# Two ternary feed-forward loops: one slot list, source order on four engines, squares moved to GpSimd and ACT, the norm's root mean square from its variance

## The chip, the cores and the metric

The kernel runs on one core of one Trainium2 chip. The time is the device time of one execution in microseconds (us). Four executions of the kernel before took 2186.79, 2187.14, 2192.76 and 2193.71 us, a median of 2189.95. A further execution was recorded by the hardware profiler; it took 2197.59 us. The engines are named as in the profile: PE (TensorE, matmuls), DVE (VectorE), ACT (ScalarE), POOL (GpSimd) and SP (SyncE, which here only issues DMAs). "PEld" is PE's loading of weights.

## The reference

`x` is 2048 tokens by 256 in float32. The reference adds eight layers to it, one after the other, each of them on the layer norm of `x`: four rounds of an attention over a context of 1601 rows and a feed-forward layer. Two of the four feed-forward layers have ternary weights, and these two are the case.

The second round's (L1, `ffn1` in the kernel):

```
def _bitlinear(x, w_latent):
    scale = jnp.clip(jnp.mean(jnp.abs(w_latent), axis=1, keepdims=True), 1e-05, None)
    tern = jnp.clip(jnp.round(w_latent / scale), -1.0, 1.0)
    ...
    return x @ (w * scale).T
h = _bitlinear(x, w_fc) + gate * (x @ v.T @ fast_b.T @ u.T)
r = jnp.maximum(h, 0.0)
return _bitlinear(r * r, w_proj)
```

It goes from 256 to 1024 columns and back, with a term of rank 16 in the first product and a squared relu between the two.

The third round's (L2, `ffn2`):

```
def _ternary_linear(x, w):
    ...
    rms = jnp.sqrt(jnp.sum(x * x, axis=-1, keepdims=True)) / jnp.sqrt(jnp.asarray(d, x.dtype))
    x_norm = x / (rms + EPS)
    return jnp.einsum('bsd,fd->bsf', x_norm, w_q)
h = jax.nn.gelu(_ternary_linear(x, w_up), approximate=False)
return _ternary_linear(h, w_down)
```

The same sizes; each of the two products first divides its input's rows by their root mean square (EPS is 1e-8). What the layer receives is already the layer norm `(x - mean) / sqrt(var + 1e-5)`. So the root mean square of the first product's input is close to one, and it follows from the variance: the mean square of a normed row is `var / (var + 1e-5)`.

## The kernel before

**Chunks and slots.** The tokens stay in SBUF as 16 tiles of 128 x 256. Both layers work through four chunks of 512 tokens (four tiles). Inside a chunk a loop runs over the 1024 hidden columns, two blocks of 128 at a time: four passes, which this text calls slots. A slot has an *up* part and a *down* part. Up multiplies the normed chunk (columns on the partitions) by the weights of two blocks into a PSUM tile of two banks (`psc`, two such tiles); then come the nonlinearity and the split of its result; down multiplies the split result back to 256 columns and adds it into two PSUM banks (`pa`, two such banks) that collect a whole chunk.

**The split.** The matmuls here take their operands in a rounded float32 form (`F32R`, fp32r in the profile). To keep the precision, a value is split into its rounded form `hi` and the rest `lo`, and each product is done for both. `parts` (L1101) splits the hidden values: ACT writes `rhi` (L1106), then DVE writes `rlo` (L1107) as the difference. The norm's output is split in the same way into `xnhi` (ACT, L179) and `xnlo` (DVE, L180). So an up has eight matmuls of 512 columns in `ffn2` (L1174), and ten in `ffn1` (L1078 and, for the term of rank 16, L1082); a down has sixteen of 256 columns (L1115).

**The norm** (`norm_steps`, L133) of a chunk takes DVE's statistics of four tiles (`bn_stats`, `bn_aggr`, L139 and L140), POOL's reciprocal root of the variance (an add L144 and a pow L145 on 128 x 4), DVE's four `xn` (L151), PE's eight transposes (L173), and the split. It is a generator: it yields at several points, so that a caller may spread it over a loop with `step(gen, n)`; `norm` (L126) runs it to its end at once. With `rms=True`, which only `ffn2` asks for, ACT squares the four `xn` with a row sum (L161), POOL and DVE make the inverse root of it (`rms_inverse`, L185: a pow, a scale, a DVE reciprocal), and DVE multiplies the four `xn` by it (L164).

**ffn1's loop** (from L1066). After an up, ACT takes the relu of the two halves (L1085), DVE squares the result in place (L1086), and `parts` splits it. The down of a slot is issued when more than two slots are waiting for theirs; the downs left over are issued at the end of the chunk. The next chunk's whole norm and its product of rank 16 (`low_rank`, L1047: eight matmuls L1052, two ACT copies, one DVE difference, `y4`) are issued behind the up of the second slot. At the end of the chunk DVE scales the four tiles of the accumulators (L1098, `y1`, three buffers) and POOL adds them to `x` (L1099).

**ffn2's loop** (from L1162). After an up, ACT takes the gelu of both halves (L1179) and `parts` splits it. DVE squares it (L1183 for the first slot, in place at L1185 for the others), and POOL sums the squares of the slots (L1186). The downs and the next norm are issued as in `ffn1`. At the end of the chunk eight matmuls against a column of ones sum the squares over the partitions (L1197), DVE copies the sums (L1202), `rms_inverse` inverts their root, and DVE scales the accumulators and adds them to `x` in one operation a tile (L1206).

**What sets the order.** The program is written in a framework that schedules each engine's instructions by priority from a planned timeline, and inserts the semaphores. `tc.manual_schedule(engines=...)` keeps the engines that it names to the order of the source for the instructions inside it. Before the change both layers name PE alone:

```
s.enter_context(tc.manual_schedule(engines={mybir.EngineType.PE}))
```

DVE, ACT and POOL are then ordered by the planner; instructions of other stages, which are outside, may stand between theirs. Each engine executes its queue in order.

Of the kernel before, what the change touches and what calls it, by code (L numbers as in the profile page):

```python
# [8 lines left out]
F32 = mybir.dt.float32  # L9
BF16 = mybir.dt.bfloat16  # L10
F32R = mybir.dt.float32r
AF = mybir.ActivationFunctionType
ALU = mybir.AluOpType
AX = mybir.AxisListType

P = 128
D = 256
IN_ORDER = {mybir.EngineType.PE, mybir.EngineType.Activation, mybir.EngineType.DVE, mybir.EngineType.Pool}
# [3 lines left out]
CH = 512  # L22
NCH = NTOK // CH
TPC = CH // P
# [16 lines left out]
def drain(gen):  # L41
    if gen is not None:
        for _ in gen:
            pass


def step(gen, n):
    if gen is None:
        return
    for _ in range(n):  # L50
        if next(gen, True):
            return


class Net:
# [77 lines left out]
    def norm_steps(self, c, out, row_scale=None, rms=False, split=None):  # L133

        nc = self.nc
# [9 lines left out]
        nc.gpsimd.tensor_tensor(rstd, rstd, self.mhalf, ALU.pow)  # L145
        if row_scale is not None:
            nc.gpsimd.tensor_tensor(rstd, rstd, row_scale, ALU.mult)
        xns = []
        for i in range(TPC):
            xn = self.xnp.tile([P, D], F32, name="xn", bufs=4)  # L150
# [3 lines left out]
            xns.append(xn)  # L154
            if i == 1:
                yield
        if rms:
            ss = self.small.tile([P, TPC], F32, name="ss")
            for i in range(TPC):
                sq = self.xnp.tile([P, D], BF16, name="sq", bufs=1)  # L160
                nc.scalar.activation(sq, xns[i], AF.Square, accum_out=ss[:, i : i + 1])  # L161
            ri = self.rms_inverse(ss, D)
            for i in range(TPC):
                nc.vector.tensor_scalar(xns[i], xns[i], ri[:, i : i + 1], None, ALU.mult)  # L164
        yield
        if split is None:
            xnT = self.xnp.tile([P, 2, CH], F32, name="xnT")
# [789 lines left out]
    def ffn1(self):  # L957
# [7 lines left out]
        with ExitStack() as s:  # L965
# [81 lines left out]
            def low_rank(hi, lo):  # L1047
# [11 lines left out]
                nc.vector.tensor_tensor(y4[64:P], ps[64:P], top[64:P].bitcast(F32), ALU.subtract)  # L1059
                return y4  # L1060

            def inputs(c):
                hi, lo = self.norm(c, split=hp)
                return hi, lo, low_rank(hi, lo)

            s.enter_context(tc.manual_schedule(engines={mybir.EngineType.PE}))  # L1066
            nxt = inputs(0)
            for c in range(NCH):
                hi, lo, y4 = nxt
                acc = [self.pa() for _ in range(2)]  # L1070
                late = []
                for f in range(0, NF, 2):
                    ps = self.psc()
                    for k in range(2):
                        fs = slice((f + k) * P, (f + k + 1) * P)
                        for kc in range(2):
                            for n, part in enumerate((hi, lo)):
                                nc.tensor.matmul(  # L1078
                                    ps[:, k, :], lhsT=wfT[:, kc, fs], rhs=part[:, kc, :],
                                    start=kc == 0 and n == 0, stop=False,  # L1080
                                )
                        nc.tensor.matmul(ps[:, k, :], lhsT=b4[:, fs], rhs=y4, start=False, stop=True)  # L1082
                    r = tp.tile([P, 2, CH], F32, name="r1")
                    for k in range(2):
                        nc.scalar.activation(r[:, k, :], ps[:, k, :], AF.Relu, scale=sc1[:, f + k : f + k + 1])  # L1085
                    nc.vector.tensor_tensor(r, r, r, ALU.mult)  # L1086
                    parts = self.parts(hp, r)
                    late.append((f, parts))
                    if len(late) > 2:
                        self.down(acc, *late.pop(0), wpT, NF)  # L1090
                    if f == 2 and c + 1 < NCH:
                        nxt = inputs(c + 1)
                for f, parts in late:
                    self.down(acc, f, parts, wpT, NF)
                for i in range(TPC):
                    x = self.x[c * TPC + i]
                    y = tp.tile([P, D], F32, name="y1")
                    nc.vector.tensor_tensor(y, acc[i // 2][:, i % 2 * D : (i % 2 + 1) * D], scb, ALU.mult)  # L1098
                    nc.gpsimd.tensor_tensor(x, x, y, ALU.add)  # L1099

    def parts(self, pool, r):  # L1101

# [19 lines left out]
    def ffn2(self):  # L1122
        tc, nc, a = self.tc, self.nc, self.a
        F = 1024
# [6 lines left out]
        with ExitStack() as s:  # L1131
# [27 lines left out]
            wdT = pool.tile([P, NF, D], F32R, name="wdT")  # L1159
            self.transpose_down(wdT, tdn)  # L1160

            s.enter_context(tc.manual_schedule(engines={mybir.EngineType.PE}))  # L1162
            nxt = self.norm(0, rms=True, split=hp)
            for c in range(NCH):
                hi, lo = nxt
                acc = [self.pa() for _ in range(2)]
                sq = hp.tile([P, 2, CH], F32, name="sq2")
                late = []
                for f in range(0, NF, 2):
                    ps = self.psc()  # L1170
                    for k in range(2):
                        for kc in range(2):
                            for n, part in enumerate((hi, lo)):
                                nc.tensor.matmul(  # L1174
                                    ps[:, k, :], lhsT=wuT[:, kc, (f + k) * P : (f + k + 1) * P], rhs=part[:, kc, :],
                                    start=kc == 0 and n == 0, stop=kc == 1 and n == 1,
                                )
                    h = tp.tile([P, 2, CH], F32, name="h2")
                    nc.scalar.activation(h, ps, AF.Gelu)  # L1179
                    parts = self.parts(hp, h)  # L1180

                    if f == 0:
                        nc.vector.tensor_tensor(sq, h, h, ALU.mult)  # L1183
                    else:
                        nc.vector.tensor_tensor(h, h, h, ALU.mult)  # L1185
                        nc.gpsimd.tensor_tensor(sq, sq, h, ALU.add)  # L1186
                    late.append((f, parts))
                    if len(late) > 2:
                        self.down(acc, *late.pop(0), wdT, NF)
                    if f == 2 and c + 1 < NCH:  # L1190
                        nxt = self.norm(c + 1, rms=True, split=hp)
                for f, parts in late:
                    self.down(acc, f, parts, wdT, NF)
                ps = self.pm()
                for i in range(TPC):
                    for k in range(2):
                        nc.tensor.matmul(  # L1197
                            ps[:, i : i + 1], lhsT=sq[:, k, i * P : (i + 1) * P], rhs=self.ones[:, 0:1],
                            start=k == 0, stop=k == 1,
                        )  # L1200
                ss = self.small.tile([P, TPC], F32, name="ss2")
                nc.vector.tensor_copy(ss, ps[:, :TPC])  # L1202
                ri = self.rms_inverse(ss, F)
                for i in range(TPC):
                    x = self.x[c * TPC + i]
                    nc.vector.scalar_tensor_tensor(  # L1206
                        x, acc[i // 2][:, i % 2 * D : (i % 2 + 1) * D], ri[:, i : i + 1], x, ALU.mult, ALU.add
                    )


    def attention3(self):
# [583 lines left out]
```

## Time and profile before

| what | value |
|---|---|
| median of four executions | 2189.95 us |
| profiled execution, its own time | 2197.59 us |
| its span, first to last instruction | 2195.9 us |
| mean granted PE clock | 0.944 of full |
| busy in the span: PE, DVE, ACT, POOL | 1939.2, 1202.6, 715.8, 629.8 us |
| relus of `ffn1` (L1085), first and last start | 1233.5 and 1325.0 us |
| gelus of `ffn2` (L1179), first and last start | 1637.2 and 1729.6 us |
| ACT's squares in the norm (L161) | 16, median 418 ns, and 187 ns each for reading the sum |
| DVE's squares, `ffn1` (L1086) and `ffn2` (L1185) | 16, median 1225 ns; 12, 1212 to 3317 ns |
| POOL's sums of squares (L1186) | 12, 2338 to 3257 ns |

How to read it: a line such as `L1086 DVE TENSOR_TENSOR r<-r 128x1024 f32` names the line of the kernel, the engine, the operation, and the tiles that it writes and reads. Times in the timeline are from the span's start. In a table of waits, "PE pm L1052 <- DVE xnlo L180: 13.0, 4, 4.1" says that PE's instructions of line 1052 waited 13.0 us in total, in 4 places, at most 4.1 us, for what DVE does in line 180. In a table of stretches a row gives its length, the busy time and number of instructions of each engine, and then the clock that was granted to PE, as a share of full. A matmul's duration reaches beyond the start of the next one, since they are pipelined; the distance of starts is what counts.

### The profile page before, as it was taken

The numbers are of one execution on the slowest core, as the hardware profiler recorded it, in microseconds if no ns is written. First come the engines' busy times: TensorE is split into PE (matmuls) and PEld (weight loads), VectorE is DVE, ScalarE is ACT, GpSimd is POOL, SyncE is SP. The second block draws the span as 40 slices with busy tenths as digits, with TensorE's granted clock in tenths as the row PEclk, the third lists the DMA queues.
The fourth block names the chain that finished last, engine by engine and source line by source line (L and its number), as shares of the span: only waits on it lengthen the run. The fifth ranks groups of instructions, "written<-read, shape, count | busy, mean of one in ns | idle before, by whom it ended". The sixth has DMA issues, their size and how long they took to land.

```text
span 2195.9 us, 22805 instructions
## 1 busy us (share of the span) xinstructions
PE 1939.2 (88%) x8841; PEld 965.5 (44%) x8841; DVE 1202.6 (55%) x2252; ACT 715.8 (33%) x968; POOL 629.8 (29%) x405
## 2 busy tenths in 40 slices
PE   7789999999998587789898789999977879888899
PEld 3223333333333533234444575455566622333487
DVE  4655655556462499985645553322156558677400
ACT  4544434444443100000011443111133246555422
POOL 1168878778686000000000111000013300111210
PEclk9799999999998599999999799999988889999999
DMA  8820000000000000000200100000000000000261
GB/s 283 274 77 1 1 1 1 1 1 1 1 1 1 0 1 0 1 0 0 67 1 2 39 1 22 1 0 1 0 1 1 5 1 1 1 1 1 102 203 62
DMA packets 39698, 63.51 MB, mean 29 GB/s; under 512 B 5133, under 2 KB 32158, under 8 KB 39582
## 3 DMA queue, kind: packets, MB, share of 16 engines
q1 hardware_dynamic: 37776, 60.33, 8.4%
q10 hardware_dynamic: 1806, 1.64, 0.2%
q8 instruction: 71, 1.16, 0.2%
q14 instruction: 45, 0.37, 0.1%
HBM read 59.87 MB, written 2.10 MB: 28 GB/s over the span
## 4 chain that ended last, share of the span: by engine, by line
PE 66%; DVE 20%; ACT 5%; issue 4%; DMA 3%; POOL 2%; SPq 0%; ACTq 0%; DVEq 0%; POOLq 0%
PE pa L468 7%; PE psc L456 5%; PE psc L641 5%; PE psc L780 4%; PE pa L800 4%; DVE ge L590 4%; DVE mp L381 4%; PE psc L1578 3%; DVE ge L592 3%; PE psc L1716 3%; PE pa L1727 3%; DVE ri L418 2%; ACT p L1585 2%; PE psc L454 2%; PE pm L376 2%
## 5 line engine op out<-in xcount | busy, mean ns | idle before, releaser
L477 POOL TENSOR_TENSOR sp<-sp,p 128x1024 f32<-128x1024 f32 (+1 forms) x176 | 419.0, 2381 | 62.4 <-ACT p L461 51.9
L381 DVE TENSOR_REDUCE mp<-pm 128x1 f32<-128x512 f32 x384 | 242.8, 680 | 162.5 <-PE pm L376 161.8
L461 ACT ACTIVATE p<-psc 128x1024 f32<-128x1024 f32 (+1 forms) x208 | 212.9, 1024 | 261.4 <-PE psc L456 162.2
L456 PE MATMUL psc<-qT,kT 64*128 64x512 f32 (+1 forms) x832 | 220.2, 592 | 0.0
L468 PE MATMUL pa<-p,v 128*64 128x512 f32 (+1 forms) x832 | 202.8, 609 | 0.0
L607 PE MATMUL psc<-ge,pick 128*8 128x512 bf16 x512 | 142.3, 378 | 37.8 <-DVE ge L590 19.0
L1585 ACT ACTIVATE p<-psc 100x1024 f32<-100x1024 f32 x128 | 124.0, 1022 | 75.8 <-PE psc L1578 73.1
L1564 DVE TENSOR_REDUCE ms<-psc 128x2 bf16<-128x800 f32 x128 | 122.7, 981 | 43.3 <-PE psc L1560 41.4
L376 PE MATMUL pm<-kb,qb 64*128 64x512 bf16 x384 | 100.4, 391 | 29.8 <-DVE mp L381 28.3
L144 POOL TENSOR_SCALAR rstd<-mv 128x4 f32<-128x4 f32 x32 | 8.7, 273 | 358.8 <-DVE mv L140 358.8
L641 PE MATMUL psc<-w_e,xe 128*128 128x512 f32 x256 | 110.4, 593 | 0.0
L468 PEld LDWEIGHTS pa<-p,v 128*64 128x64 f32 (+1 forms) x832 | 50.9, 137 | 133.9 <-issue 130.8
L843 POOL MEMSET v<- 128x4 f32 x1 | 0.1, 105 | 365.9 <-DVE n_odd L294 365.9
L780 PE MATMUL psc<-q,kT 128*128 128x512 f32 (+1 forms) x208 | 102.2, 610 | 0.0
L590 DVE TENSOR_SCALAR ge<-bc,g 128x128 bf16<-128x128 f32 (+15 forms) x128 | 100.2, 783 | 1.8 <-ACT bc L584 1.8
L456 PEld LDWEIGHTS psc<-qT,kT 64*128 64x128 f32 (+1 forms) x832 | 85.4, 185 | 19.9 <-issue 6.6
L800 PE MATMUL pa<-v,p 128*128 128x257 f32 (+1 forms) x416 | 93.9, 381 | 0.0
L607 PEld LDWEIGHTS <-pick 128*8 128x8 bf16 x512 | 39.4, 85 | 117.2 <-issue 91.2
L592 DVE TENSOR_SCALAR ge<-bc,g 128x1920 bf16<-128x1920 f32 (+14 forms) x120 | 89.8, 750 | 1.0 <-ACT bc L584 1.0
L753 DVE TENSOR_REDUCE mp<-pm 128x1 f32<-128x512 f32 x64 | 34.4, 571 | 99.8 <-PE pm L748 99.7
L454 PE MATMUL psc<-sh,negz 64*128 64x512 bf16 (+1 forms) x416 | 87.1, 384 | 1.1 <-ACT sh L403 0.7
L648 DVE SCALAR_TENSOR_TENSOR x<-psc,g,x 128x256 f32<-128x256 f32 x128 | 61.9, 484 | 46.1 <-PE psc L641 42.6
(343 smaller groups left out, 3268.3 us busy)
## 6 DMA issues: line engine op xcount, KB each, us to landing
w<-in_L_ffn_w_dram SPq DMA_DIRECT2D x16, 1024.0 KB, 7.5
head<-in_mask_BxSxS_ik_dram SPq DMA_DIRECT2D x16, 600.5 KB, 4.4
head<-in_mask_1x1xSxS_ik_dram SPq DMA_DIRECT2D x16, 600.5 KB, 4.9
tail<-in_mask_BxSxS_ik_dram SPq DMA_DIRECT2D x16, 200.0 KB, 4.1
tail<-in_mask_1x1xSxS_ik_dram SPq DMA_DIRECT2D x16, 200.0 KB, 4.3
x<-in_x_dram SPq DMA_DIRECT2D x16, 128.0 KB, 3.4
w_e<-in_L_ffn_experts_dram SPq DMA_DIRECT2D x2, 1024.0 KB, 7.1
out_dram<-y SPq DMA_DIRECT2D x16, 128.0 KB, 2.3
```

Source lines behind the costliest of these rows:

```text
L381: nc.vector.tensor_reduce(mp[:, i, j, n : n + 1], pair[j][:, :wd], AX.X, ALU.max)
L456: nc.tensor.matmul(sc[:r, j, :], lhsT=kT[h, hp, kt * P : kt * P + r], rhs=q[h, :], start=False, stop=True,)
L461: nc.scalar.activation(p[:r], sc[:r], AF.Exp, scale=DH**-0.5)
L468: nc.tensor.matmul(acc[h, :], lhsT=v[:r, kt, hp * P + h.start : hp * P + h.stop], rhs=p[:r, j, :], start=kt == 0, stop=kt == NKT - 1,)
L477: nc.gpsimd.tensor_tensor(sums[:r], sums[:r], p[:r], ALU.add)
L590: nc.vector.tensor_scalar(ge[:, :hi], bc[:, :hi], own, None, ALU.is_lt)
L592: nc.vector.tensor_scalar(ge[:, hi:], bc[:, hi:], own, None, ALU.is_le)
L607: nc.tensor.matmul(rk[j // 2][0:E, j % 2, :], lhsT=pick[:, e, :], rhs=ge[:, j * CH : (j + 1) * CH], start=first, stop=last,)
L641: nc.tensor.matmul(sc[:, j, :], lhsT=xnT[t // TPC][:, kc, (t % TPC) * P : (t % TPC + 1) * P], rhs=ew[kc][:, half * 4 + 2 * j : half * 4 + ...
L780: nc.tensor.matmul(sc[:r, j, :], lhsT=kT[:, kc, ks], rhs=q[:, kc, :], start=kc == 0, stop=False)
L800: nc.tensor.matmul(acc[:, : D + 1], lhsT=p[:r, kt, i * P : (i + 1) * P], rhs=v[:r, kt, :], start=kt == 0, stop=kt == NKT - 1,)
L1585: nc.scalar.activation(p[:TR], sc[k][:TR], AF.Exp, scale=DH**-0.5)
```

## The change

Both loops are rewritten as one list of sixteen slots over all chunks, with the order of the source kept on PE, ACT, DVE and POOL (`IN_ORDER`):

- The down of slot n is issued behind the up of slot n+2, over the ends of chunks too, where before the chunk's end issued all that was left.
- The next chunk's norm is a generator that is created at the first slot of a chunk and stepped by three yields at the end of each slot: statistics and the reciprocal root in the first; `xn`, and transposes, in the first and second; what is left in the third (in `ffn1` the product of rank 16).
- In `ffn1` the square goes from DVE to POOL, and a slot's split is issued at the start of the next slot, ahead of that slot's relu. `y1` has four buffers.
- In `ffn2` the squares of the gelu go from DVE to ACT, into a tile of their own (`hh`); POOL's sum stays.
- The norm's root mean square comes from the variance on POOL, on 128 x 4 values, and goes into `rstd` before `xn` is made; ACT's squares of `xn` and DVE's second multiplication are gone.

The core of the diff:

```
+        if rms:
+            ms = self.small.tile([P, TPC], F32, name="ms")
+            nc.gpsimd.tensor_tensor(ms, rstd, rstd, ALU.mult)
+            nc.gpsimd.tensor_tensor(ms, ms, mv[:, :, 1], ALU.mult)
+            ri = self.rms_inverse(ms, 1)
+            nc.gpsimd.tensor_tensor(rstd, rstd, ri, ALU.mult)
+            yield
         xns = []
...
-        if rms:
-            ss = self.small.tile([P, TPC], F32, name="ss")
-            for i in range(TPC):
-                sq = self.xnp.tile([P, D], BF16, name="sq", bufs=1)
-                nc.scalar.activation(sq, xns[i], AF.Square, accum_out=ss[:, i : i + 1])
-            ri = self.rms_inverse(ss, D)
-            for i in range(TPC):
-                nc.vector.tensor_scalar(xns[i], xns[i], ri[:, i : i + 1], None, ALU.mult)
...
-            s.enter_context(tc.manual_schedule(engines={mybir.EngineType.PE}))
+            s.enter_context(tc.manual_schedule(engines=IN_ORDER))
```

`ffn1`'s loop as it is after the change:

```
+            drain(inputs(0))
+            slots = [(c, f) for c in range(NCH) for f in range(0, NF, 2)]
+            squares, late, accs = [], [], {}
+            nxt = None
+            for n in range(len(slots) + 2):
+                if squares:
+                    c, f, r = squares.pop(0)
+                    late.append((c, f, self.parts(hp, r)))
+                if n < len(slots):
+                    c, f = slots[n]
+                    ps = up(c, f)
+                    r = tp.tile([P, 2, CH], F32, name="r1")
+                    for k in range(2):
+                        nc.scalar.activation(r[:, k, :], ps[:, k, :], AF.Relu, scale=sc1[:, f + k : f + k + 1])
+                    nc.gpsimd.tensor_tensor(r, r, r, ALU.mult)
+                    squares.append((c, f, r))
+                    if f == 0:
+                        nxt = inputs(c + 1) if c + 1 < NCH else None
+                if n >= 2:
+                    c, f, parts = late.pop(0)
+                    if f == 0:
+                        accs[c] = [self.pa() for _ in range(2)]
+                    self.down(accs[c], f, parts, wpT, NF)
+                    if f == NF - 2:
+                        for i in range(TPC):
+                            outputs(c, i, accs[c])
+                step(nxt, 3)
```

`inputs(c)` runs `norm_steps`, yields, and then does the product of rank 16; `up(c, f)` holds the matmuls of an up, and `outputs(c, i, acc)` the two operations of a tile's output. In `ffn2` the loop has the same form; the body of a slot and the end of a chunk are:

```
+                    h = tp.tile([P, 2, CH], F32, name="h2")
+                    nc.scalar.activation(h, ps, AF.Gelu)
+                    late.append((c, f, self.parts(hp, h)))
...
+                    if f == 0:
+                        sqs[c] = hp.tile([P, 2, CH], F32, name="sq2")
+                        nc.scalar.activation(sqs[c], h, AF.Square)
+                        nxt = inputs(c + 1) if c + 1 < NCH else None
...
+                        h2 = tp.tile([P, 2, CH], F32, name="hh")
+                        nc.scalar.activation(h2, h, AF.Square)
+                        nc.gpsimd.tensor_tensor(sqs[c], sqs[c], h2, ALU.add)
...
+                    self.down(accs[c], f, parts, wdT, NF)
+                    if f == NF - 2:
+                        ri = inverse(sqs.pop(c))
+                        for i in range(TPC):
+                            x = self.x[c * TPC + i]
+                            nc.vector.scalar_tensor_tensor(
+                                x, accs[c][i // 2][:, i % 2 * D : (i % 2 + 1) * D], ri[:, i : i + 1], x,
+                                ALU.mult, ALU.add,
+                            )
+                step(nxt, 3)
```

`inverse(sq)` holds the eight matmuls of the sums, the copy, and `rms_inverse`, which before stood at the end of the chunk's loop. The sequence of PE's instructions is the same as before outside these two loops.

## The prediction

> **What bounds the kernel now.** I read the page's totals first: TensorE (PE) is busy for 88% of the span, so the time is PE's work plus PE's waits. The order of PE's instructions in the built changed kernel differs only inside the loops of `ffn1` and `ffn2`; so I read, second, the busy time in those two stretches (columns: length, then busy us and count of PE, PEld, DVE, ACT, POOL, granted clock):
>
> ```profile
> 1222.00:1336.00 114.00, 94.60 (x498) 79.09 (x496) 64.88 (x108) 48.41 (x72) 19.58 (x25) 0.89 0.01 1
> 1636.00:1750.00 114.00, 93.05 (x491) 80.79 (x490) 73.60 (x106) 43.75 (x63) 45.45 (x32) 0.81 0.01 3
> ```
>
> PE is idle for 40 us in the two, and part of the rest runs at a lowered clock. Third, what PE waits for in them (total us, times, longest):
>
> ```profile
> PE pm L1052 <- DVE xnlo L180: 13.0, 4, 4.1
> PE pa L1115 <- DVE rlo L1107: 3.6, 5, 0.9
> ...
> PE pm L1197 <- POOL sq L1186: 13.0, 4, 3.8
> PE pa L1115 <- DVE rlo L1107: 5.2, 7, 2.4
> PE pm L173 <- DVE xn L164: 2.6, 2, 1.7
> ```
>
> So `ffn1` waits for the low part of the next chunk's norm, `ffn2` for the last square's sum at a chunk's end. Fourth, DVE and POOL in order of time (start, us):
>
> ```profile
> 1650.28 1.21 DVE L1107 TENSOR_TENSOR rlo<-h,rhi 128x1024 fp32r<-128x1024 f32 x1
> 1651.53 3.30 DVE L1185 TENSOR_TENSOR h<-h 128x1024 f32<-128x1024 f32 x1
> ...
> 1672.13 2.77 DVE L151 TENSOR_SCALAR xn<-x,mv,rstd 128x256 f32<-128x256 f32 x3
> ...
> 1678.02 0.39 DVE L139 BATCH_NORM_STATS2 st<-x 128x6 f32<-128x256 f32 x1
> ```
> ```profile
> 1650.50 3.24 POOL L1186 TENSOR_TENSOR sq<-sq,h 128x1024 f32<-128x1024 f32 x1 [2.69 <-DVE h L1185]
> ...
> 1671.69 2.40 POOL L1186 TENSOR_TENSOR sq<-sq,h 128x1024 f32<-128x1024 f32 x1 [8.35 <-DVE h L1185]
> ```
>
> These carry the case. A POOL add that wants to start at 1650.50, while DVE's `rlo` runs, takes 3.24 us instead of 2.35 and ends 2.3 after `rlo`; DVE's square, ready at 1651.53, takes 3.30 instead of 1.22 and ends 1.1 after the add. So large DVE operations with their inputs in SBUF and POOL's large ones exclude each other, and the one that has waited goes next. `xn` is held too (first of three, until 1674.09); the statistics (0.39 inside an add at 1677.63) and what reads PSUM are not. Fifth, the chain at the end of `ffn1`:
>
> ```profile
> 1324.45 1.28 ACT r L1085 x2
> 1325.75 1.24 DVE r L1086
> 1327.01 1.06 ACT rhi L1106
> 1328.09 1.24 DVE rlo L1107
> 1329.37 1.11 PE pa L1115 x7
> ```
>
> **The change, part by part.** I call U(n) the end of slot n's `up` (four slots a chunk); relu or gelu starts there. Before, U(0), U(4), U(8), U(12) are at 1233.4, 1260.4, 1287.2, 1314.7 and the last `down` ends at 1330.5; in `ffn2` they are at 1637.1, 1664.2, 1693.2, 1721.6 and the last sums end at 1743.8. I walk the new queues with the old rows: `up` 10 x 0.233 = 2.33 in `ffn1`, 8 x 0.233 = 1.87 in `ffn2`, `down` 16 x 0.118 = 1.9, low rank 1.9, four transposes 0.52; ACT: relu pair 1.28, `rhi` 1.05, `xnhi` 0.59; DVE: `rlo` 1.22, four statistics 2.1, `xn` 0.35; POOL: full-size operation 2.35, pow 1.04.
>
> Part 1, squares of `ffn1` to POOL. No row squares a tile there; between the one-input CAST (L686, 0.62 for 512 columns, so 1.24) and the two-input TENSOR_TENSOR (L477, 2.35) I take 2.35, the same operation. Since `rhi` of slot n-1 stands before relu(n) on ACT, a ring closes: 1.28 + 2.35 + 1.05 and hops = 4.85 us a slot, against PE's 4.23.
>
> Part 2, the order. Before, the next chunk's statistics and `xn` ran early; now they queue behind `rlo` on DVE, and the transposes stand in PE's order before the `up` of slot 2. Chunk 0 of `ffn1`: relu(0) 1233.4-34.7, its square to 37.15, pow to 38.6, `xn` 0 and 1 to 39.35, `rlo`(0) to 40.55; the square of slot 1, waiting since 39.6, goes next, to 42.95; `xn` 2 and 3 to 43.65. PE, done with slot 1 at 35.75, waits 7.9 for them. After such a wait its clock is low. Bound from below: after 4.1 us idle before 1240.76 the matmuls stood 0.43 apart for 3.3 us; from above: 5.0 us, from 1225.9 on. I take 5.0 behind waits over 6, as PE's work had been thin for long there too, and 3.3 behind shorter ones. Transposes to 45.6, `up`(2) to 49.35, then `down`, low rank, `up`, `down`, `up` = 10.36: U(4) = 1259.7, a chunk of 26.3 against 27.0. Chunk 1: statistics behind `rlo`(3), then square, pow, `rlo`(4), the square of slot 5 until U(4)+9.95, one `xn`, one x add (0.74), the other: transposes done at +12.1 (PE idle about 4.5), U(6) +16.0, U(8) +26.3 (26.8 before). Chunk 2 also holds the next stage's statistics and pow, which the new order interleaves: +1.3, 27.6 (27.5 before). Last chunk: nothing but the ring and four x adds in POOL's queue (2.95) with `rlo` between: the square of slot 15 ends at U(12)+20.35, `rhi` 21.45, `rlo` 22.7, `down` 24.6, against 15.8 before. The sum is -0.7 -0.5 +0.1 +8.8 = +7.7; four y buffers and no statistics between the y's give 0.8 back: **+6.9**.
>
> Part 3, `ffn2`. ACT's squares (1.03, as a gelu) cost nothing while PE covers them: gelu, `rhi`, square = 3.1 of PE's 3.77 a slot; uncovered, 16 of them would be 16.5. DVE loses 4 x 1.22 a chunk, ACT 4 x 0.6 and DVE 4 x 0.35 of the old norm. But the norm's chain is now in series behind `rlo`: statistics 2.1, then on POOL add 0.23, pow 1.04, two multiplies, pow 1.01, scale 0.19, reciprocal 0.18 on DVE. The multiplies of 128x4 have no row: from 0.19 (L190) to 1.04 (L145); I take 0.21, nearest L190, since L1099's 0.74 at 256 columns against 2.35 at 1024 leaves 0.2 at few. With hops 3.5. Behind that reciprocal stand `rlo`(1) and then `xn`: chunk 0: gelu 1637.15, `rhi` to 39.2, `rlo` 40.4, statistics 42.5, chain 46.05, `rlo`(1) 47.4, the waiting POOL add to 49.8, `xn` 51.2. PE has been idle since U(1) = 39.0, so 12.2 us; low clock: `up`(2) to 55.65, then 8.35 more: U(4) = 1664.0 (1664.2 before). Chunk 1, from U(4): `rlo` 3.3, statistics 5.4, chain 8.95, `rlo`(5) 10.15; copy of the sums; POOL's add 12.55, then the inverse of chunk 0 behind it (pow, scale, reciprocal) 14.15, four outputs on DVE 15.8, `xn` 17.2. PE has ended `down` and the sums by 8.2 and waits 9.0; U(6) 21.65, U(8) 30.0 (29.0 before). Chunk 2 also carries four statistics and one pow of the next stage, +2.9: 32.9 (28.4). Chunk 3 has no norm, but `down`(12) waits 1.9 for the accumulators that the inverse of chunk 2 frees: 23.3 (22.2). Sum -0.2 +1.0 +4.5 +1.1 = **+6.4**.
>
> Together +13.3. The profiled execution took 2197.6 (its span 2195.9 and 1.7 around it), 7.6 above the median of 2189.95; it becomes 2210.9, the median 2203.2. Nothing else moves: SP's queue and its DMAs keep their order, and the branch that is not taken does not run.
>
> The Trainium skill ("TensorE: Matmul & The Clock Gate", Part 1) holds that PE falls to half clock after an idle window of about 3.4 us and rises after about 3.4 us of work; the 4.1 us wait agrees, the 5.0 from 1225.9 is longer. By its 3.4 alone the sum would be 3 us lower, an estimate.
>
> Bounds: where DVE keeps the port over a waiting POOL, 6.2 less (2.35 in each first chunk and 0.75 twice); 3.3 us of low clock at the four long waits, 4 x 1.7 x 0.46 = 3.1 less; squares at 1.24, about 7.5 less (1.1 in four slots of the last chunk and once in each other). So -3.5 at the low end. Three multiplies at 1.04 in three chunks, 7.5 more; hops 0.05 too short, ten a chunk, 4 more: +24.8 at the high end. Range 2186 to 2215.
>
> **The rivals.** (a) Faster: the next chunk's norm stays hidden under PE's work, as the new slots lay it out. For it: PE alone needs 4 x 19.8 = 79 and 4 x 17.9 = 72 us. Against: the walk puts 4.5 to 12 us of wait before six sets of transposes. It decides from 3.3 us a wait: if the six are each 3.3 shorter, 20 us go and 2183 stands; if all their 47 us go, 2156. (b) No change: squares at the one-input price and DVE keeping the port: about 13.3 - 7.5 - 6.2, with the clock at its low end 2187 to 2190. (c) Worse: the small multiplies cost as much as pow: 2211.
>
> **How the numbers follow.** A measurement tells 0.3%, 6.6 us. My case 0.52 (own range 2197 to 2209), (c) 0.12, (b) 0.21, (a) 0.15. Slower: (c), and nine tenths of mine: 0.59; same: (b) and the rest of mine, 0.26; faster 0.15. Range 2186 to 2215 leaves out (a) and a tail.
>
> **What would show it.** Right: before `up`(2) of each chunk with a norm to come, PE waits for `xn` (L173 <- DVE L159) 4 to 12 us, six times, at low clock after; POOL's squares begin when `rlo` ends; the waits L1052 <- `xnlo` and sums <- `sq` are gone; last `down` of `ffn1` near U(12)+24. Wrong: transposes that start within 2 us of the `up` before them; squares of 1.3; `rlo` inside a square at 1.22.

## The result

| | before | after |
|---|---|---|
| median time | 2191.51 us (78 runs, 2183.26 to 2198.42) | 2194.29 us (51 runs, 2188.67 to 2201.5) |
| ratio, with its 95% interval | | 1.0015 (1.0009 to 1.0021) |
| profiled execution, its span | 2197.59, 2195.9 us | 2194.53, 2192.8 us |
| `ffn1`, from L992's start to the next layer's first matmul of L692 | 135.7 us | 133.0 us |
| `ffn2`, from its thresholds' first reduction to the next layer's transposes of L1503 (L1545 in after) | 132.9 us | 137.1 us |
| mean granted PE clock | 0.944 | 0.943 |

The change makes the kernel slower by 0.15%, which is real over so many runs, but within the 0.3% that the forecast called no change. The forecast said 0.6% slower. The profiled execution of before lay 6 us above its median, that of after at its median; 3.0 us of the difference of the traces are there before `ffn1` begins, where no code differs. So the two traces are compared by the length of a stage, not by the span: `ffn1` became 2.7 us shorter, `ffn2` 4.2 longer; the stretch between them is 0.5 shorter, the one behind them 1.2.

In what follows the lines of after are L1079/L1083 for `ffn1`'s up, L1107 relu, L1108 square, L1127 `rhi`, L1128 `rlo`, L1136 down, L159 `xn`, and for `ffn2` L1197 up, L1226 gelu, L1235 square on ACT, L1236 POOL's sum, L1208 sums, L1246 outputs.

The same two stretches of after (columns as before: length, then busy us and count of PE, PEld, DVE, ACT, POOL, clock):

```profile
1222.00:1336.00 114.00, 96.95 (x495) 79.35 (x495) 54.34 (x116) 47.55 (x71) 54.51 (x48) 0.88 0.04 11
1636.00:1750.00 114.00, 83.52 (x486) 72.67 (x487) 46.97 (x100) 50.58 (x59) 51.66 (x47) 0.80 0.01 3
```

DVE is busy for 10 and 27 us less, and in `ffn2` PE does less in the same stretch, not more. What PE waits for there (total us, times, longest), first `ffn1`, then `ffn2`:

```profile
PE pm L173 <- DVE xn L159: 11.7, 7, 2.9
...
PE pm L1052 <- DVE xnlo L180: 0.5, 1, 0.5
...
PE pm L173 <- DVE xn L159: 31.8, 3, 12.4
PE pa L1136 <- DVE x L1246: 2.6, 1, 2.6
```

The two waits of 13.0 us that led the table before are gone (`xnlo` 0.5, the sums none), and one for `xn`, before the transposes of the next chunk, stands in their place: smaller than the old one in `ffn1`, more than twice as large in `ffn2`. Why `xn` is late is seen on DVE and POOL in order of time, in chunk 0 of each loop:

```profile
1235.45 1.22 DVE L1128 TENSOR_TENSOR rlo<-r,rhi 128x1024 fp32r<-128x1024 f32 x1
1236.59 2.31 DVE L159 TENSOR_SCALAR xn<-x,mv,rstd 128x256 f32<-128x256 f32 x2
...
1636.53 0.18 DVE L140 BATCH_NORM_AGGREGATE mv<-st 128x2 f32<-128x6 f32 x1
1640.10 0.18 DVE L192 RECIPROCAL rmsi<-rms 128x4 f32<-128x4 f32 x1 [3.39 <-POOL rms L190]
1640.19 1.19 DVE L1128 TENSOR_TENSOR rlo<-h,rhi 128x1024 fp32r<-128x1024 f32 x1
1641.48 3.37 DVE L159 TENSOR_SCALAR xn<-x,mv,rstd 128x256 f32<-128x256 f32 x4
```
```profile
1231.56 1.89 POOL L1108 TENSOR_TENSOR r<-r 128x1024 f32<-128x1024 f32 x1 [38.00 <-ACT r L1107]
...
1235.77 2.65 POOL L1108 TENSOR_TENSOR r<-r 128x1024 f32<-128x1024 f32 x1 [1.00 <-ACT r L1107]
...
1638.50 0.20 POOL L152 TENSOR_TENSOR ms<-ms,mv 128x4 f32<-128x4 f32 x1
...
1640.36 1.08 POOL L154 TENSOR_TENSOR rstd<-rstd,rmsi 128x4 f32<-128x4 f32 x1 [0.30 <-DVE rmsi L192]
1641.40 2.34 POOL L1236 TENSOR_TENSOR sq<-sq,hh 128x1024 f32<-128x1024 f32 x1
```

In `ffn2` DVE idles 3.39 us in the middle of the chain while POOL works on 128 x 4 values; then `rlo`, which stands ahead of `xn` in the source, runs; then four `xn` take 3.37 us, since a POOL addition that had waited went first. The first line of POOL is the surprise: an undisturbed square takes 1.89 us, where the forecast had 2.35. PE in the same chunk:

```profile
1644.03 1.35 PE L173 MATMUL pm<-ident,xn 128*128 128x128 f32 x4 [12.38 <-DVE xn L159]
...
1647.32 0.63 PE L1197 MATMUL psc<-xnlo,wuT 128*128 128x512 f32 x1
1647.75 0.51 PE L1197 MATMUL psc<-xnhi,wuT 128*128 128x512 f32 x1
1648.09 0.39 PE L1197 MATMUL psc<-xnlo,wuT 128*128 128x512 f32 x1
```

After 12.4 us idle the matmuls stand 0.43 apart instead of 0.23, until 4.1 us from the first transpose; behind the waits of the next two chunks (8.8 and 10.7 us) this lasts 6.1 and 5.5 us. The transposes begin when the first of the four `xn` is done, not the last. The chain at the end of `ffn1`:

```profile
1318.90 1.27 ACT r L1107 x2
...
1320.24 1.90 POOL r L1108
...
1322.16 1.05 ACT rhi L1127
...
1323.24 1.24 DVE rlo L1128
...
1324.52 1.11 PE pa L1136 x7
```

It has the form that the forecast gave it, with POOL's square in DVE's place, at 1.90.

### The profile page after: what moved, and what is told of

It reads as the page before. It is cut to its first block, busy times and chain, and to the rows that moved or that the text cites. A ratio compares the mean times of both kernels' runs of the same rounds, so it can differ in the third digit from the quotient of the medians.

```text
span 2192.8 us, 22772 instructions
## 1 busy us (share of the span) xinstructions
PE 1925.6 (88%) x8841; PEld 956.7 (44%) x8841; DVE 1153.9 (53%) x2204; ACT 723.5 (33%) x952; POOL 661.3 (30%) x433
## 4 chain that ended last, share of the span: by engine, by line
PE 65%; DVE 18%; ACT 5%; issue 4%; POOL 4%; DMA 3%; SPq 0%; ACTq 0%; DVEq 0%; POOLq 0%
PE pa L468 7%; PE psc L456 5%; PE psc L641 5%; PE psc L780 4%; PE pa L800 4%; DVE ge L590 4%; PE psc L1620 3%; DVE mp L381 3%; DVE ge L592 3%; PE psc L1758 3%; PE pa L1769 3%; DVE ri L418 2%; ACT p L1627 2%; PE pm L173 2%; PE psc L454 2%
## 5 line engine op out<-in xcount | busy, mean ns | idle before, releaser
L173 PE MATMUL pm<-ident,xn 128*128 128x128 f32 x256 | 47.6, 325 | 51.0 <-DVE xn L159 43.5
L1662 POOL TENSOR_TENSOR attn<-o,ri 128x512 f32<-128x512 f32 x16 | 20.3, 1271 | 228.9 <-DVE ri L1660 207.7
```

## The experiments

Every run below is compared with the kernel before on the same chip. The stage columns are from one profiled execution each, measured as in the table above, so a microsecond or two of them is chance; the ratios are from repeated runs.

| run | ffn1 | ffn2 | median us | ratio to before (95%) |
|---|---|---|---|---|
| before | 135.7 | 132.9 | 2191.5 | 1 |
| after | 133.0 | 137.1 | 2194.3 | 1.0015 (1.0009 to 1.0021) |
| `ffn1` alone | 132.9 | 132.5 | 2186.8 | 0.9982 (0.9965 to 1.0) |
| `ffn2` and norm alone | 135.0 | 136.3 | 2194.6 | 1.0021 (1.0007 to 1.0035) |
| two operands for POOL's square | 139.0 | 137.2 | 2204.0 | 1.0055 (1.004 to 1.007) |
| norm's mean square alone | 134.9 | 129.6 | 2187.4 | 0.9983 (0.9971 to 0.9995) |
| PE kept busy | 132.2 | 133.8 | 2185.7 | 0.9974 (0.9962 to 0.9985) |
| DVE, ACT, POOL planned | 117.7 | 105.5 | 2145.8 | 0.9795 (0.9771 to 0.982) |
| DVE alone planned | 129.3 | 110.6 | 2166.1 | 0.9885 (0.9868 to 0.9903) |
| statistics first | 114.5 | 109.2 | 2142.4 | 0.9786 (0.976 to 0.9812) |
| planned and statistics first | 117.7 | 108.0 | 2147.4 | 0.9801 (0.9783 to 0.9819) |
| mixed by stage | 114.0 | 105.8 | 2141.3 | 0.9782 (0.9766 to 0.9799) |
| planned, all squares on DVE | 112.1 | 113.0 | 2150.3 | 0.9802 (0.9783 to 0.9821) |
| planned, `ffn1`'s squares on DVE | 112.1 | 103.3 | 2134.1 | 0.9743 (0.9719 to 0.9766) |

**The parts by themselves.** Two kernels take the change apart by stage: the new `ffn1` with the old `ffn2` and norm, and the reverse. Their edits are the hunks of the change itself.

> The changed ffn1 alone; ffn2 and the norm stay as they were before. The forecast's sum for this part was +6.9 us against the kernel before. The theory after the traces: the square of POOL costs 1.89 us and not 2.35, and less time at low clock follows a chunk's wait, so ffn1 is shorter by 2.7 us (135.7 to 133.0): -2 to -3.5 us against before, a ratio of 0.9984 to 0.9991. Rival: the traces' difference of ffn1 is the difference of two executions and the part is worth nothing or a loss: 0 to +3 us.

> The changed ffn2 and the norm's root mean square alone; ffn1 stays as it was before. The forecast's sum for this part was +6.4 us. The theory: +4 to +5 us against before (stage 132.9 to 137.1 in the traces), a ratio of 1.0018 to 1.0023. Rival: the two parts are not separate (a shift of one stage changes the other): this run and the one of ffn1 alone then do not add up to the changed kernel's +3 us within 1.5 us.

Measured: -0.18% (the interval ends at no change) and +0.21%. That is -3.9 and +4.6 us, against the forecast's +6.9 and +6.4. The first is a little below its theory's range, and its rival keeps only the end of the interval; the second is in its theory's range. Their sum, +0.7, misses the changed kernel's +3 by more than the 1.5 us that the rival set, but the two intervals together allow 5 us either way, so the times do not decide whether the parts are separate. The stage columns speak for it: each stage, old or new, has within 1 us the same length beside the old other stage as beside the new one. The forecast of `ffn2` stands within the interval (its 6.4 is 0.29%); that of `ffn1` has the wrong sign. Most of the error lies in `ffn1`.

**The price of POOL's square.** The multiplication is kept, but its second input is another tile, of ones; so this kernel leaves out the squaring.

```
+            unit = pool.tile([P, 2, CH], F32, name="unit")
+            nc.gpsimd.memset(unit, 1.0)
...
-                    nc.gpsimd.tensor_tensor(r, r, r, ALU.mult)
+                    nc.gpsimd.tensor_tensor(r, r, unit, ALU.mult)
```

> The changed kernel, but POOL multiplies the relu by a tile of ones in place of itself in ffn1, so that its two inputs are different tiles, as the forecast's row for the price had them (2.35 us). The squaring is left out by this. Theory (two reads of one tile cost 1.89 us, two tiles 2.35, and the last chunk's ring goes by that difference): POOL's multiplication 2.33 to 2.41 us, the last chunk's period 21.7 to 23.5 us, the others up by 0.5 to 2.5 us, in all +4 to +8 us against the changed kernel, a ratio to before of 1.003 to 1.005. Rival (the price does not matter, since PE's waits for the norm set the period): within 1.5 us of the changed kernel, a ratio of 1.001 to 1.002, even with multiplications of 2.35.

The line's instructions in this kernel, and in after (least, median and greatest ns):

```profile
L1110 POOL TENSOR_TENSOR r<-r,unit x16: 2357/2402/3162, 1228.7 to 1322.3; 128x1024 f32<-128x1024 f32 x16
```
```profile
L1108 POOL TENSOR_TENSOR r<-r x16: 1893/1894/2987, 1231.6 to 1320.2; 128x1024 f32<-128x1024 f32 x16
```

The same operation on the same shape takes 2.40 us with two tiles and 1.89 with one tile given twice. The time rises to 1.0055, 0.40% or 8.8 us over the changed kernel (the two intervals together allow 3.5 either way), `ffn1` by 6.0 us in the trace. The loop of `ffn1` by chunks, from the first relu of one to that of the next, and in the last to the end of the last down:

| | chunk 0 | 1 | 2 | 3 | sum |
|---|---|---|---|---|---|
| forecast, at 2.35 a square | 26.3 | 26.3 | 27.6 | 24.6 | 104.8 |
| this run, at 2.40 | 26.1 | 25.3 | 26.7 | 24.9 | 103.0 |
| after, at 1.89 | 23.5 | 25.65 | 25.4 | 21.8 | 96.4 |
| before, DVE's square | 26.9 | 26.8 | 27.6 | 16.7 | 98.0 |

With the forecast's price in the kernel, the forecast's walk comes out within 1.0 us in each chunk and 1.8 over the four. Against before this run is 12 us slower by its ratio (9 to 15 by the interval), where the forecast had 13.3; its two stages in the trace show 7.6 of that. The time and the last chunk are a little over the theory's range; the rival, that the price would not matter, falls.

**The norm's part alone.** In the kernel before, only the root mean square is taken from the variance (the first two hunks of the change).

> The kernel before with one part alone: the norm's root mean square from its variance. Theory: ACT's 16 squares with row sums (0.6 us each) and DVE's 16 second multiplications (0.35 each) go, but both were off the path but for the 2.6 us that the transposes waited for line 164: -1 to -4 us against before, a ratio of 0.998 to 0.9995. Rival: the planner, with DVE and ACT freed, starts the next norm earlier and the waits at a chunk's end shrink with it: -8 us or more, a ratio below 0.9965.

Measured 0.9983, 3.7 us; the theory's range holds it, and the rival is outside the interval. The stage of `ffn2` is 3.3 us shorter.

**Is it the order?** The changed kernel with one word different in each loop: the planner orders DVE, ACT and POOL again.

```
-            s.enter_context(tc.manual_schedule(engines=IN_ORDER))
+            s.enter_context(tc.manual_schedule(engines={mybir.EngineType.PE}))
```

> The changed kernel, but in the two loops only PE keeps the source's order; DVE, ACT and POOL are ordered by the planner as before the change. Theory (the source's order puts the next chunk's norm in series behind the splits of the hidden values): the waits of the transposes for xn (11.7 us in ffn1, 31.8 in ffn2) mostly go, and with them the low clock behind them: 25 to 35 us faster than the changed kernel, a ratio to before of 0.985 to 0.990. Rival (the port that DVE and POOL share and POOL's longer work make the wait, whatever the order): within 6 us of the changed kernel, a ratio of 0.999 to 1.004.

It is 45 us faster than before and 48 faster than the changed kernel, more than the theory had. PE's waits in its two loops, `ffn1` first:

```profile
PE pm L1052 <- DVE xnlo L180: 2.7, 4, 0.9
...
PE pa L1136 <- DVE x L1246: 5.7, 3, 2.5
PE pa L1136 <- DVE rlo L1128: 1.9, 2, 1.0
```

No transpose waits for `xn` (43.5 us in the two loops of after), and the clock rises with it. The busy times and the clock in this kernel's two loops, and then in after's (the second stretch of after holds less than three of its chunks, that of the planned kernel nearly all four):

```profile
1222.00:1314.00 92.00, 83.84 (x481) 72.07 (x482) 51.06 (x88) 44.73 (x67) 50.78 (x39) 0.97 0.00 1
1614.00:1690.00 76.00, 68.23 (x434) 61.34 (x433) 43.22 (x61) 51.77 (x55) 39.94 (x23) 0.96 0.00 1
```
```profile
1222.00:1314.00 92.00, 79.41 (x407) 66.97 (x407) 45.92 (x95) 40.87 (x59) 42.72 (x35) 0.87 0.00 1
1630.00:1710.00 80.00, 48.19 (x269) 42.01 (x268) 32.94 (x74) 35.20 (x38) 31.88 (x34) 0.74 0.00 1
```

POOL and ACT do the same work with the same squares as in after, and POOL is as busy or busier; so neither the squares' new places by themselves nor that large operations of DVE and POOL exclude each other makes the wait: the order does.

**Which queue?** DVE alone is given to the planner; ACT and POOL keep the source's order.

```
+            s.enter_context(tc.manual_schedule(engines=IN_ORDER - {mybir.EngineType.DVE}))
```

> The changed kernel, but in the two loops DVE alone is ordered by the planner; PE, ACT and POOL keep the source's order. It asks in which queue the norm's chain stands behind other work. Theory (DVE's: statistics and xn behind rlo of the slot): nearly all that the fully planned version gains, 35 to 47 us faster than the changed kernel, a ratio to before of 0.980 to 0.986. Rival 1 (POOL's: the pow and the inverse behind the squares and sums): less than 10 us gained, above 0.997. Rival 2 (both queues about equally): 15 to 30 us, 0.988 to 0.995.

28 us of the 48: the theory misses, and the time is in the range of the rival of both queues. The stages differ, though: `ffn2` gets back 26.5 of the 31.6 us that the full plan gives it, `ffn1` 3.7 of 15.3. POOL in chunk 1 of this kernel's `ffn1`, and then in chunk 1's turn of its `ffn2`:

```profile
1262.28 1.89 POOL L1108 TENSOR_TENSOR r<-r 128x1024 f32<-128x1024 f32 x1 [2.34 <-ACT r L1107]
1264.14 0.23 POOL L144 TENSOR_SCALAR rstd<-mv 128x4 f32<-128x4 f32 x1
1264.45 1.04 POOL L145 TENSOR_TENSOR rstd<-rstd,mhalf 128x4 f32<-128x4 f32 x1
```
```profile
1646.31 2.43 POOL L1236 TENSOR_TENSOR sq<-sq,hh 128x1024 f32<-128x1024 f32 x1 [1.02 <-ACT hh L1235]
1648.83 0.23 POOL L144 TENSOR_SCALAR rstd<-mv 128x4 f32<-128x4 f32 x1
1649.14 1.04 POOL L145 TENSOR_TENSOR rstd<-rstd,mhalf 128x4 f32<-128x4 f32 x1
```

In `ffn1` POOL's add and pow stand behind the square of the slot, and `xn` follows at 1265.53, with PE still waiting 10.1 us for it over the loop. In `ffn2` DVE has made this chunk's statistics before the loop, but POOL's add and pow stand behind the sum of the last slot (1646.31), and `xn` follows at 1652.62. So DVE's queue held most in `ffn2`; what is left fits POOL's queue, but ACT keeps its order here too, and no run plans POOL alone.

**Ahead of the loop.** The source's order stays on four engines, but the statistics and inverse roots of all four chunks are made before each loop, so a chunk's first slot holds only `xn`, and its second the transposes.

```
+            pre = [self.norm_stats(c, rms=True) for c in range(NCH)]
...
-                yield from self.norm_steps(c, out, rms=True, split=hp)
+                yield from self.norm_ready(c, out, pre[c], hp)
```

> The changed kernel, but the statistics and the inverse roots of all four chunks are made ahead of each loop; a chunk's first slot holds only the four xn, its second the transposes. (The values are the same: the statistics of a chunk are those of x before the loop.) Theory (the wait is for the chain statistics, pow, mean square, pow, reciprocal behind rlo, and xn at its end): the transposes wait less than 2 us a chunk; some 5 us are added ahead of each loop; the six waits of 43 us and the low clock behind them go but for that: 20 to 40 us faster than the changed kernel, a ratio to before of 0.983 to 0.992. Rival (xn waits for the port behind POOL's additions, whatever stands ahead of it): less than 10 us gained, a ratio above 0.997.

51.9 us faster than the changed kernel, more than the theory had. The longest waits of PE in its `ffn2` (L1183 is the down there, L1294 the outputs, L211 and L221 a chunk's `xn` and transposes; in `ffn1` none for the norm is left):

```profile
PE pa L1183 <- DVE x L1294: 6.5, 3, 2.6
PE pm L221 <- DVE xn L211: 2.4, 1, 2.4
```

So the order of the source is not bad as such: an order in which the chain is not in series costs as little as the planner's. The rival's "less than 10 us" falls. But the edit also frees `xn` of POOL's additions: it is now ready a slot earlier, and four take 1.4 us behind `rlo`(0), from 1614.18 on, with the next addition at 1616.99. In after, the first `xn` was held for 2.0 us of PE's 12.4; so the additions were a part of the wait, and the chain the larger one.

**Together, and by stage.** Two runs ask whether the two cures add.

> Both edits of the two fastest runs together: the planner's order for DVE, ACT and POOL in the two loops, and all statistics ahead of each loop. Theory (both remove the same waits, so they do not add): within 6 us of either (2145.84 and 2142.44 us), a ratio to before of 0.976 to 0.981. Rival (each left something that the other removes): below 0.975.

> By stage, the better of the two: ffn1 in the source's order with its statistics ahead of the loop (stage of 114.5 us in the traces, planned 117.7), ffn2 planned, with its statistics in the loop (105.6 us, the other 109.2). Theory (the stages are separate and add): 3 us below the planned version and 4 below the other, so 2139 to 2143 us, a ratio to before of 0.976 to 0.979. Rival: the stage lengths of single traces differ by chance, and nothing is gained over 2142.44.

They do not add (2147.4 us), as the theory had it. The mixed version is at 2141.3; its interval overlaps those of both parents, so its gain of 1.1 and 4.5 us over them is not decided.

**What the squares are worth.** In the planned version both loops' squares go back to DVE, and then only `ffn1`'s.

```
-                    nc.gpsimd.tensor_tensor(r, r, r, ALU.mult)
+                    nc.vector.tensor_tensor(r, r, r, ALU.mult)
```

> The changed kernel with the planner's order for DVE, ACT and POOL in the two loops (as in the run before, 2145.84 us), and the squares back on DVE in both: the square of ffn1 in place, the squares of the gelu into their own tile. It asks how much of the 45 us that the planned version stands below the kernel before comes from moving the squares. Theory (PE bounds these loops once its waits are gone; DVE then has some 2.5 of a slot's 4.2 us, and what it has besides can hide): +2 to +10 us against the planned version, a ratio to before of 0.980 to 0.984; the gain comes from the list of slots. Rival (DVE was the bound, and its relief is the gain): +20 us or more, a ratio above 0.989.

> The planned version (2145.84 us) with ffn1's square back on DVE; the squares of ffn2 stay on ACT. In the traces the planned stage of ffn1 is 112.1 us with the square on DVE and 117.7 with it on POOL; that of ffn2 is 113.1 with DVE's squares and 105.6 with ACT's. Theory (the move to POOL costs in ffn1 and the move to ACT gains in ffn2): 4 to 6 us faster than the planned version, 2140 to 2142 us, a ratio to before of 0.976 to 0.978. Rival (the two stage lengths differ by chance, and the move is worth nothing in ffn1): 2144 to 2148 us, 0.979 to 0.981.

With all squares on DVE the time is 4.4 us higher by the medians and 1.5 by the ratios, whose intervals overlap: moving both together is worth little or nothing. So the gain over the kernel before comes from the rest of the change under the planner's order: the list of slots with its downs across the ends of chunks, the norm in steps, and the root mean square from the variance (3.7 us alone in the kernel before); no run separates the first two. But each move counts, and they go against each other. With only `ffn1`'s squares on DVE the kernel is at 2134.1 us, 0.9743, the fastest of all and 60 us below the changed kernel. It is 13 us below the version with all squares on DVE by the ratios (the intervals allow 7 either way), so ACT's squares are a gain in `ffn2` (stage 113.0 to 103.3); and it is 12 us below the planned version, twice what the stage lengths promised, so POOL's are a loss in `ffn1`. ACT's `rhi` in `ffn1` of the planned version, and of this one (busy us, mean ns, then the idle time before it and what ended it):

```profile
L1127 ACT CAST rhi<-r 128x1024 fp32r<-128x1024 f32 x16 | 16.8, 1050 | 35.4 <-POOL r L1108 35.4
```
```profile
L1108 DVE TENSOR_TENSOR r<-r 128x1024 f32<-128x1024 f32 x16 | 20.1, 1257 | 5.6 <-ACT r L1107 5.1
L1127 ACT CAST rhi<-r 128x1024 fp32r<-128x1024 f32 x16 | 16.8, 1053 | 15.0 <-DVE r L1108 15.0
```

DVE's square takes 1.26 us against POOL's 1.9, and DVE, busy for 64 of the 92 us from 1222 on, has room for it. `ffn1` is 5.6 us shorter and `ffn2`, with the same code in both, 2.3; the rest of the 12 is in no stage that these edits touch, and within what the intervals allow (7 either way).

**The clock.** Matmuls that nobody reads are put into PE's queue in place of most of the wait for `xn` in `ffn2`.

```
+                if nxt is not None and n < len(slots) and slots[n][1] == 2:
+                    ps = self.pm()
+                    for k in range(48 if n == 1 else 34):
+                        nc.tensor.matmul(ps, lhsT=wuT[:, 0, 0:P], rhs=wuT[:, 0, 0:CH], start=True, stop=True)
```

> The changed kernel with work added that nobody reads: 48 matmuls of 512 columns in PE's queue ahead of the first transposes of ffn2's chunk 0, and 34 each in chunks 1 and 2, which fill most of the time in which PE waits for xn there (12.4, 9.7 and 9.7 us in the trace). Theory (the up behind such a wait runs at low clock: 4.45 to 4.87 us where a warm one takes 2.4 from its transposes' start, three times, and the down(12) case beside it): 4 to 8 us faster than the changed kernel, a ratio to before of 0.998 to 0.9996. Rival (the low clock behind the waits costs nothing on the path, since DVE and POOL set the next step): within 1.5 us of the changed kernel, 1.001 to 1.002.

```profile
1626.04 11.04 PE L1253 MATMUL pm<-wuT 128*128 128x512 f32 x48
1638.62 1.21 PE L173 MATMUL pm<-ident,xn 128*128 128x128 f32 x4 [1.54 <-DVE xn L159]
1639.59 0.48 PE L1197 MATMUL psc<-xnhi,wuT 128*128 128x512 f32 x1
1639.91 0.40 PE L1197 MATMUL psc<-xnlo,wuT 128*128 128x512 f32 x1
1640.14 0.39 PE L1197 MATMUL psc<-xnhi,wuT 128*128 128x512 f32 x1
```

The waits before `xn` become 1.5 and 1.1 us in chunks 0 and 1, and behind the first of these waits the matmuls stand 0.23 apart from the second matmul on. From the first transpose to the end of `up` it takes 3.05 us in chunks 0 and 1 (4.45 and 4.86 in after); in chunk 2 3 us of wait were left, and it took 4.47 (4.87 in after). That makes 3.6 us, and the stage is 3.3 shorter. The time is lower by 0.41% of before, 9 us (the intervals allow 3 either way). That is more than either theory had. The low clock behind the waits costs, then; but of the 9 us the trace shows a third where the edit is, and where the rest lies was not found.

## Why the prediction was wrong, point by point

- **Part 1, the price of the square: wrong, and it is the step that failed.** Between a one-input and a two-input row the forecast took the upper end, "2.35, the same operation": the operation was the same, but its operands were not. One tile given twice took 1.89 us. The bounds (1.24 to 2.35) held it; the choice within them did not. The ring of a slot (relus, square, `rhi`) became 1.27 + 1.89 + 1.05 = 4.21 us, and 4.24 from relu to relu in the last chunk: as long as PE's 4.23, and so no cost, where 4.85 had been forecast. The run with two tiles has 4.73, and puts 6.6 us of the loop on this term, of the 8.4 by which the forecast was too long there.
- **Part 2, the order in `ffn1`: the walk was right, its sum not.** Of the 1.8 us left, chunks 1 and 2 have 1.0 and 0.9, the ends cancel. The trace has the walk's order: two `xn`, `rlo`(0), the next square, two `xn`. With both squares shorter the last `xn` ended 8.7 us after the first relu's start, not 10.25; PE's wait of 7.9 us fell into two (2.9 and 2.6), and the up(2) behind them took 3.4 us where 3.75 were forecast. One reading was wrong: the last down of before ends at 1331.4, not 1330.5. The chain that the forecast read shows the seven matmuls that the first output waits for; the last of the sixteen is this one:

```profile
1331.15 0.28 PE L1115 MATMUL pa<-wpT,rlo 128*128 128x256 f32 x1
```

  So the forecast's loss in the last chunk was 0.9 us too large. The tail after the last down lost 0.85 us where 0.8 was charged.
- **Part 3, `ffn2`: right in its mechanism and near in its size, in part by luck.** Periods of 25.3, 29.5, 31.3 and 25.1, sum 111.1, where 26.9, 30.0, 32.9 and 23.3, sum 113.1, were forecast; against before (106.6) that is +4.5, not +6.4. PE waited 12.4 us in chunk 0 where 12.2 were forecast, but both ends of this wait came earlier than in the walk: up(1) ended 0.4 us after the first gelu's start, not 1.9 (a table load of 1.28 us stands before that gelu), and the transposes began 12.8 us after it, not 14.1, since they wait for the first `xn` and the walk had them wait for the fourth; in chunk 1 16.1, not 17.2. The low clock behind the three waits lasted 4.1, 6.1 and 5.5 us, where 5.0 was taken. Against these gains the last chunk was 1.8 longer, since its down waited 2.6 us, not 1.9, and then ran at low clock, which was not charged (3.2 us instead of 2.1, and the up behind it 2.55 instead of 2.0).
- **The small multiplies:** 0.20 us, where 0.21 was taken. Rival (c) is gone; but one of them took 1.08 while `rlo` ran.
- **"The one that has waited goes next":** right in both loops (`xn` 2.31 behind a square, 3.37 for four behind an addition). So rival (b) came true in its outcome and half in its reasons: the squares were cheaper, though not at the one-input price, and DVE did not go on before a waiting POOL.
- **Rival (a), the norm hidden:** not in this kernel. Its size was about right: the forecast had 2156 if all 47 us of waits went; with the chain out of series, by the planner or ahead of the loop, 2146 and 2142 were measured. What the forecast did not ask is which of the changed things keeps the waits; it was the fixed order, on DVE above all in `ffn2`.
- **The signs to look for:** the old waits are gone and the new one is there, in `ffn1` in shorter pieces than "4 to 12 us"; the squares of 1.3 did not come; the last down of `ffn1` ended at U(12) + 21.8, not 24. The profiled execution of before was 6 us above its median, and the forecast's difference was rightly set on the median.

In the place of the failed step: a square of 1.89 us, which makes `ffn1` 6.6 us shorter than one of 2.40. By the stages of the traces the forecast was 9.6 us too high in `ffn1` (+6.9 forecast, -2.7 measured) and 2.2 in `ffn2` (+6.4 and +4.2); of the 9.6, 6.6 are the square, 1.8 the rest of the walk and 0.9 the misread end. By the medians it was 10.5 too high in all (+13.3 and +2.8).

## What to carry to other kernels

A duration is taken over from a row only if the operands agree too, the number of different tiles among them; where the price decides whether a ring is above or below the bound of the bottleneck engine, both ends of its bounds should be walked through, not one. Where an order is fixed by the source, the first question is which short chain (statistics, root, reciprocal, scale) then runs in series behind large operations, on every engine that it crosses; making it a stage ahead was worth 52 us here, and leaving the order to the planner 48. A change that moves the time little can hold a gain of 2% and a loss of 2%: the change gave 45 us under the planner's order, and the fixed order took them back.

## What the runs showed of the hardware

- GpSimd's product of a tile with itself took 1.89 us for 128x1024 in float32, of two tiles 2.40.
- A multiply of 128x4 on GpSimd, 0.20 us by itself, took 1.08 while DVE's `rlo` ran, and ended 0.06 us behind it: small operations are held as well.
- PE's clock fell after shorter idleness than the 4.1 us that the forecast had read: in the planned version a wait of 2.5 us, behind an up that followed the sums of one column, was followed by 3.1 us of matmuls of 256 columns 0.21 apart, where they stand 0.12 apart otherwise:

```profile
1633.75 1.84 PE L1208 MATMUL pm<-ones,sq 128*128 128x1 f32 x16
...
1640.46 0.55 PE L1136 MATMUL pa<-wdT,rhi 128*128 128x256 f32 x1 [2.52 <-DVE x L1246]
...
1641.03 0.42 PE L1136 MATMUL pa<-wdT,rhi 128*128 128x256 f32 x1
1641.24 0.41 PE L1136 MATMUL pa<-wdT,rlo 128*128 128x256 f32 x1
...
1643.66 0.28 PE L1136 MATMUL pa<-wdT,rlo 128*128 128x256 f32 x1
```

  In `ffn1` of after, chunk 1, it fell with no one-column matmul near: behind a full down, waits of 2.44 and 0.26 us with the transposes of `xn` around them were followed by 4.8 us at half the pace:

```profile
1262.52 0.47 PE L173 MATMUL pm<-ident,xn 128*128 128x128 f32 x1 [2.44 <-DVE xn L159]
...
1266.08 0.63 PE L1083 MATMUL psc<-y,b 128*128 128x512 f32 x1
1266.51 0.63 PE L1079 MATMUL psc<-xnhi,wfT 128*128 128x512 f32 x1
```

  The Trainium skill ("TensorE: Matmul & The Clock Gate", Part 1) gives an idle window of about 3.4 us for that. Both rows have less idleness than that; whether one-column matmuls or transposes count toward the window, no run here tells apart.
